# Turning x on VectorE and by DMA instead of on TensorE ahead of an attention layer, with pairs of batches sharing q and k

## The chip, the cores and the metric

The kernel runs on one core of a Trainium2 chip. The metric is the time of one execution in device microseconds (us); times below are medians of several executions. Profiles are single executions of the same programs. An engine's queue that issues transfers is written with a q: SPq is the queue of SyncE, which issues nearly all DMA transfers here, one after the other and in the order of the program.

## The reference, cut to what matters

128 batches of 128 nodes with 512 features (fp32) go through four graph layers, each with a residual and a normalisation. Layer 2 needs x in rows; layer 3 is masked attention with 8 heads, and needs x turned, features on the partitions, for its products with `w_qkv`.

```python
x = _layernorm(x + L0(x))             # adj @ x @ weight + bias
x = _layernorm(x + L1(x))             # graph attention
x = _layernorm(x + L2(x))             # max over nodes
qkv = (x @ w_qkv).reshape(b, n, 3, H, hd).transpose(2, 0, 3, 1, 4)   # layer 3
attn = softmax(where(mask == 0, -inf, q @ k.T * scale))
o = (attn @ v) @ w_proj + b_proj
x = _layernorm(x + o + layernorm(o) * gamma + beta)
```

## The kernel before

A batch is a chain of steps written as a Python generator. A small scheduler (`Plan`) knows a modelled duration of each step and the number of buffers of each kind, and emits the instructions in the order in which its model says they can start; so the order on every engine is fixed when the kernel is built, and a wrong modelled duration gives an order in which something waits. Ranks decide between steps that could start together; the last four batches are ranked 16 ahead, so that they do not end together with nothing beside them.

The steps that matter: layer 3's x is turned on TensorE, four 128x128 transposes per batch, and copied out by ScalarE. Four batches (`G`) share a tile `xT`, so that a q or k product has 512 columns.

```python
G = 4
BUFS = {..., "xT": 1, "v": 8, "qkT": 2, "pr": 2, "pt": 1, "prT": 2, ...}
...
    def query_key(gr, c):                  # 8 of these per group
        yield gr.turned
        ...
        p = product(lambda k: wqkv_sb[:, k, c * P : (c + 1) * P], lambda k: gr.xT[:, k, :])
...
    def batch(i):
        ...                                # layers 0 to 2
        p = bank([P, K, P], "tr")
        for k in range(K):
            nc.tensor.transpose(p[:, k, :], xb[:, k * P : (k + 1) * P], ident)
        yield use("ACT", 0.6, urgent=True)
        nc.scalar.copy(gr.xT[:, :, b * P : (b + 1) * P], p)
        ...
        # softmax: pr on VectorE and ScalarE, turned as 32x32 blocks into pt,
        # written to DRAM (p_d) and read back (prT) through SyncE
        scratch = dram.tile([P, Q, H * S], F32, name="p_d")
        yield use("SP", 0.1, late=2.8)
        to_rows(pt..., scratch)
        bt = yield use("SP", 0.1, "prT", late=4.0)
        from_rows(prT, scratch)
```

The softmax already uses the detour that the change gives to x: a blockwise turn on VectorE, then a DMA to DRAM and back that puts the blocks in place.

## Time and profile before

| | before |
|---|---|
| time, median of 3 | 3414.68 us (3414.14 to 3414.78) |
| TensorE busy | 3378.9 us, 99% |
| TensorE idle (span 3412.8 less busy) | 33.9 us |
| VectorE busy | 76% |
| share of the DMA engines | 19.5% |

The end of the kernel, TensorE in order of time (start us, us, what, and in brackets the idle time ahead of it and what ended it):

```profile
3378.09 1.98 PE L600 MATMUL tr<-prT,v 128*64 128x128 f32 x16 [3.13 <-DMA prT<-p_d]
3381.73 5.17 PE L195 MATMUL mm<-wproj_sb,oT 128*128 128x512 f32 x8 [1.67 <-ACT oT L609]
3388.61 3.70 PE L195 MATMUL mm<-wproj_sb,oT 128*128 128x512 f32 x8 [0.69 <-ACT oT L609]
```

The reader is to see two things: the last batches wait for their own softmax and copies, since nothing else is left to do; and after the wait of 3.13 us the same work takes longer, 5.17 us where the next eight products take 3.70.

### The profile page before, as it was taken

Reading aid. Unit: us, or ns where it says so; the run is one execution under the profiler, and the core shown is the slowest. Engines: PE = TensorE matmul, PEld = TensorE weight load, DVE = VectorE, ACT = ScalarE, POOL = GpSimd, SP = SyncE. Lnnn points to the kernel's source line nnn. Section 1 sums busy time; section 2 is a strip of 40 time slices with the busy share of each in tenths; the row PEclk is TensorE's granted clock in tenths of the full one; section 3 lists DMA queues with packets and bytes.
Section 4 is the critical chain, followed back from the end, with each engine's and each line's share of the span. In section 5 each row is a group of like instructions: output and inputs, shape, how many; then the busy total and the mean of one; then the engine's idle time right before and its main releaser. Section 6 shows DMA issues by size and latency. Waiting matters only on the chain.

```text
span 3412.8 us, 39442 instructions
## 1 busy us (share of the span) xinstructions
PE 3378.9 (99%) x13193; PEld 1727.3 (51%) x13193; DVE 2588.1 (76%) x5399; ACT 1251.9 (37%) x3585; POOL 981.2 (29%) x1031
## 2 busy tenths in 40 slices
PE   9999999999999999999999999999999999999998
PEld 5555555545455455455555555555555545555543
DVE  7776976788777787777877777877778777797766
ACT  3433343334334233342343333433324334244332
POOL 2222422223221333223332223322233222341222
PEclk9999999999999999999999999999999999999999
DMA  4022121202121122111222112221112211121112
GB/s 155 32 86 71 54 75 56 87 30 78 67 77 53 47 78 78 62 60 46 79 76 68 62 48 71 78 68 65 56 56 78 77 60 59 50 78 59 53 69 79
DMA packets 169354, 228.58 MB, mean 67 GB/s; under 512 B 43456, under 2 KB 117312, under 8 KB 169152
## 3 DMA queue, kind: packets, MB, share of 16 engines
q1 hardware_dynamic: 169152, 226.08, 19.5%
q8 instruction: 104, 1.70, 0.2%
q14 instruction: 98, 0.80, 0.1%
HBM read 116.98 MB, written 109.05 MB: 66 GB/s over the span
## 4 chain that ended last, share of the span: by engine, by line
PE 92%; DVE 7%; issue 1%; DMA 0%; ACT 0%; POOL 0%; SPq 0%; POOLq 0%; DVEq 0%; ACTq 0%
PE mm L195 73%; PE tr L203 6%; PE sc L553 4%; PE tr L600 4%; PE mm L515 3%; PE tr L534 2%; DVE st L161 1%; DVE scr L488 1%; DVE x L182 0%; DVE x L507 0%; DVE mv L163 0%; DVE x L481 0%; PE tr L380 0%; DVE x L506 0%; DVE ve L165 0%
## 5 line engine op out<-in xcount | busy, mean ns | idle before, releaser
L195 PE MATMUL mm<-w_sb,yT 128*128 128x512 f32 x2048 | 921.0, 595 | 0.5 <-ACT yT L206 0.5
L195 PE MATMUL mm<-xT,wqkv_sb 128*128 128x512 f32 x2048 | 898.7, 594 | 5.2 <-DVE x L481 2.9
L168 POOL TENSOR_TENSOR rstd<-ve,neghalf 128x1 f32<-128x1 f32 x640 | 446.4, 698 | 1268.5 <-DVE ve L165 1103.3
L195 PEld LDWEIGHTS mm<-xT,wqkv_sb 128*128 128x128 f32 x2048 | 384.7, 190 | 468.5 <-issue 447.0
L195 PEld LDWEIGHTS mm<-w_sb,yT 128*128 128x128 f32 x2048 | 375.5, 190 | 410.4 <-issue 398.1
L195 PE MATMUL mm<-wqkv_sb,xT 128*128 128x512 f32 x1024 | 467.2, 599 | 0.0
L195 PE MATMUL mm<-wproj_sb,oT 128*128 128x512 f32 x1024 | 458.1, 596 | 3.8 <-ACT oT L609 3.8
L188 POOL TENSOR_TENSOR x<-x,beta_sb 128x512 f32<-128x512 f32 x128 | 186.0, 1463 | 937.4 <-PE tr L534 937.4
L571 ACT ACTIVATE pr<-pr,nmx 128x128 f32<-128x128 f32 x1024 | 398.8, 394 | 137.3 <-DVE nmx L567 137.2
L161 DVE BATCH_NORM_STATS2 st<-x 128x6 f32<-128x512 f32 x512 | 349.9, 683 | 4.7 <-ACT x L522 3.4
L177 ACT ACTIVATE x<-x,nmr,rstd 128x512 f32<-128x512 f32 x256 | 206.0, 810 | 288.1 <-DVE nmr L175 284.2
L195 PEld LDWEIGHTS mm<-wproj_sb,oT 128*128 128x128 f32 x1024 | 191.8, 191 | 234.5 <-issue 227.6
L560 DVE TENSOR_TENSOR pr<-sc,maskb 128x1024 f32<-128x1024 f32 x128 | 156.6, 1224 | 191.0 <-PE sc L553 185.3
L195 PEld LDWEIGHTS mm<-wqkv_sb,xT 128*128 128x128 f32 x1024 | 187.0, 190 | 208.7 <-issue 200.6
L442 DVE COPY qkT<-mm 128x512 f32<-128x512 f32 x128 | 87.3, 682 | 247.4 <-PE mm L195 247.2
L206 ACT COPY yT<-tr 128x512 f32<-128x512 f32 x256 | 148.3, 584 | 292.6 <-PE tr L203 290.8
L188 POOL TENSOR_TENSOR x<-x,o 128x512 f32<-128x512 f32 x128 | 180.2, 1408 | 153.6 <-DVE o L617 153.1
L440 ACT ACTIVATE qkT<-mm 128x512 f32<-128x512 f32 x128 | 75.4, 589 | 383.0 <-PE mm L195 383.0
L488 DVE SCALAR_TENSOR_TENSOR scr<-x,wa_rows 128x512 f32<-128x512 f32 x256 | 200.5, 783 | 9.4 <-ACT x L177 3.0
L188 POOL TENSOR_TENSOR x<-x,bias_sb 128x512 f32<-128x512 f32 x128 | 176.7, 1387 | 67.8 <-PE tr L203 57.1
L571 ACT ACTIVATION_READ_ACCUMULATOR pr<-pr,nmx 128x1 f32 x1024 | 195.3, 191 | 0.0
L609 ACT COPY oT<-tr 128x512 f32<-128x512 f32 x128 | 75.0, 586 | 273.4 <-PE tr L600 273.2
(65 smaller groups left out, 3753.6 us busy)
## 6 DMA issues: line engine op xcount, KB each, us to landing
p_d<-pt SPq DMA_DIRECT2D x128, 512.0 KB, 2.6
prT<-p_d SPq DMA_DIRECT2D x128, 512.0 KB, 3.7
x<-in_x SPq DMA_DIRECT2D x128, 256.0 KB, 2.6
out<-x SPq DMA_DIRECT2D x128, 256.0 KB, 2.0
e_d<-et SPq DMA_DIRECT2D x64, 128.0 KB, 1.7
eT<-e_d SPq DMA_DIRECT2D x64, 128.0 KB, 2.2
wqkv_sb<-in_L_gnn_w_qkv SPq DMA_DIRECT2D x1, 3072.0 KB, 10.8
w_sb<-in_L_gnn_weight SPq DMA_DIRECT2D x1, 1024.0 KB, 5.7
```

Of the source, the lines that this page charges most:

```text
L161: nc.vector.bn_stats(st, src)
L168: nc.gpsimd.tensor_tensor(rstd, ve, neghalf, op=ALU.pow)
L177: nc.scalar.activation(xb, xb, AF.Identity, bias=nmr, scale=rstd)
L188: nc.gpsimd.tensor_tensor(dst, dst, other, op=ALU.add)
L195: nc.tensor.matmul(p, lhs(k), rhs(k), start=(k == 0), stop=(k == K - 1))
L203: nc.tensor.matmul(p[:, k, :], xb[:, k * P : (k + 1) * P], nodes, start=True, stop=True)
L206: nc.scalar.copy(yT, p)
L488: nc.vector.scalar_tensor_tensor(scr, xb, 1.0, wa_rows[:, j, :], op0=ALU.mult, op1=ALU.mult, accum_out=gr.s[:, b, j : j + 1],)
L553: nc.tensor.matmul(sc[:, j, c, :], gr.qkT[rws, c, nodes], gr.qkT[rws, K + c, nodes], start=True, stop=True,)
L560: nc.vector.tensor_tensor(pr, sc.rearrange("p j c m -> p (j c) m"), maskb[:, None, :].to_broadcast([P, H, P]), op=ALU.add,)
L571: nc.scalar.activation(pr[:, j, :], pr[:, j, :], AF.Exp, bias=nmx[:, j : j + 1], accum_out=sums[:, j : j + 1],)
L600: nc.tensor.matmul(p[j * HD : (j + 1) * HD, c, :], valued.v[:, (2 * c + j) * HD : (2 * c + j + 1) * HD], prT[:, j * K + c], start=True, st ...
```

## The change

The intent is to take 512 transposes off the engine that is busy 99% of the time. VectorE turns x as 32x32 blocks (`nc.vector.transpose`), SyncE writes the result to DRAM (256 KB) and reads it back in four transfers of 64 KB whose runs are 128 bytes; so the features arrive in another order on the partitions, and the rows of `w_qkv` are loaded in that order too. At the same time groups shrink from four batches to two: `xT` is half as large and gets two buffers, and the q and k products have 256 columns, two in one bank. The diff, cut to its core:

```diff
-G = 4
+G = 2
-    ... "xT": 1, "v": 8, "qkT": 2, "pr": 2, "pt": 1, "prT": 2, ...
+    ... "xT": 2, "v": 8, "qkT": 3, "pr": 2, "pt": 1, "xt": 2, "prT": 2, ...
-        matrix(wqkv_sb, w_qkv)
+        for q in range(Q):
+            nc.sync.dma_start(
+                wqkv_sb[q::Q], w_qkv[q * P : (q + 1) * P].rearrange("(k r) o -> r k o", r=S)
+            )
...
-        p = product(lambda k: wqkv_sb[:, k, c * P : (c + 1) * P], lambda k: gr.xT[:, k, :])
+        p = bank([P, 2, G * P], "mm")
+        for j in range(2):
+            for k in range(K):
+                nc.tensor.matmul(
+                    p[:, j, :], wqkv_sb[:, k, (c + j) * P : (c + j + 1) * P], gr.xT[:, k, :], ...)
...
+    def features(xt, bt, gr, b):
+        scratch = dram.tile([P, Q, P], F32, name="x_d", bufs=8)
+        yield use("SP", 0.1, late=2.3)
+        to_rows(xt, scratch)
+        give(bt)
+        got = yield use("SP", 2.0, lambda: () if gr.xT else ("xT",), late=5.0)
+        ...
+        for a in range(Q):
+            at = b * P + a * S
+            nc.sync.dma_start(
+                gr.xT[:, :, at : at + S],
+                scratch[a * S : (a + 1) * S].rearrange("r q (k s) -> (r q) k s", k=K),
+            )
+        done(gr.turned)
...
-        for k in range(K):
-            nc.tensor.transpose(p[:, k, :], xb[:, k * P : (k + 1) * P], ident)
-        yield use("ACT", 0.6, urgent=True)
-        nc.scalar.copy(gr.xT[:, :, b * P : (b + 1) * P], p)
+        bt = yield use("DVE", 0.65, "xt")
+        xt = buf([P, Q, P], "xt")
+        nc.vector.transpose(xt.rearrange("p q f -> p (q f)"), xb)
+        plan.start(features(xt, bt, gr, b), i)
```

More of the change, by code (lines that the diff above doesn't have):

```diff
@@ L30 @@
     "tr": 3, "mm": 3, "sc": 1,
-    "x": 16, "yT": 3, "e": 2, "et": 1, "eT": 2, "ex": 2, "xT": 1, "v": 8, "qkT": 2,
-    "pr": 2, "pt": 1, "prT": 2, "oT": 2, "o": 2,
+    "x": 16, "yT": 3, "e": 2, "et": 1, "eT": 2, "ex": 2, "xT": 2, "v": 8, "qkT": 3,
+    "pr": 2, "pt": 1, "xt": 2, "prT": 2, "oT": 2, "o": 2,
 }
@@ L273, in loads @@
         landing(bias0_in, P)
-        for i in range(2, G):
+        for i in range(2, 4):
             yield from load(i)
@@ L281, in loads @@
         plan.start(logit_rows(a_sb, slot), 0)
-        for i in range(G, 2 * G):
+        for i in range(4, 8):
             yield from load(i)
@@ L289, in loads @@
         landing(scalars_in, 2 * P)
-        for i in range(2 * G, 3 * G):
+        for i in range(8, 12):
             yield from load(i)
         yield use("SP", 2.5)
-        matrix(wqkv_sb, w_qkv)
+        for q in range(Q):
+            nc.sync.dma_start(
+                wqkv_sb[q::Q], w_qkv[q * P : (q + 1) * P].rearrange("(k r) o -> r k o", r=S)
+            )
         matrix(wproj_sb, w_proj)
@@ L297, in loads @@
         landing(w3_in, (4 * K + 3) * P)
-        for i in range(3 * G, NB):
+        for i in range(12, NB):
             yield from load(i)
@@ L351, in __init__ @@
             self.attention = [Event() for _ in range(G // 2)]
-            self.turned, self.qk = Event(G), Event(2 * K)
+            self.turned, self.qk = Event(G), Event(K)
             self.eT, self.xT, self.qkT, self.slot, self.left = {}, None, None, {}, {}
@@ L367, in group @@
                 plan.start(attention1(groups[g], h), g * G + 2 * h - (16 if g * G >= NB - 4 else 0))
-            for n in range(2 * K):
-                plan.start(query_key(groups[g], n // 2 + K * (n % 2)), g * G + n / (2 * K) - (16 if g * G >= NB - 4 else 0))
+            for n in range(K):
+                plan.start(query_key(groups[g], n // 2 * 2 + K * (n % 2)), g * G + n / K - (16 if g * G >= NB - 4 else 0))
         return groups[g]
@@ L435, in query_key @@
             bp = got
-        p = product(lambda k: wqkv_sb[:, k, c * P : (c + 1) * P], lambda k: gr.xT[:, k, :])
-        gr.read("xT", G + 2 * K)
+        p = bank([P, 2, G * P], "mm")
+        for j in range(2):
+            for k in range(K):
+                nc.tensor.matmul(
+                    p[:, j, :], wqkv_sb[:, k, (c + j) * P : (c + j + 1) * P], gr.xT[:, k, :],
+                    start=(k == 0), stop=(k == K - 1),
+                )
+        gr.read("xT", G + K)
         yield use("ACT" if c < K else "DVE", 0.69, urgent=True)
+        dst = gr.qkT[:, c : c + 2, :]
         if c < K:
-            nc.scalar.mul(gr.qkT[:, c, :], p, HD**-0.5)
+            nc.scalar.mul(dst, p, HD**-0.5)
         else:
             nc.vector.tensor_copy(
-                gr.qkT[:, c, :].rearrange("p (b c r) -> p b c r", b=G, c=Q),
-                p.rearrange("p (b r c) -> p b c r", b=G, c=Q),
+                dst.rearrange("p j (b c r) -> p (j b) c r", b=G, c=Q),
+                p.rearrange("p j (b r c) -> p (j b) c r", b=G, c=Q),
             )
@@ L459, in values @@
         give(bp)
-        gr.read("xT", G + 2 * K)
+        gr.read("xT", G + K)
         event.slot = bv
         done(event)
+    def features(xt, bt, gr, b):
[4 more added lines that the diff above has]
+        got = yield use("SP", 2.0, lambda: () if gr.xT else ("xT",), late=5.0)
+        if gr.xT is None:
+            gr.slot["xT"] = got
+            gr.xT = buf([P, K, G * P], "xT")
+        for a in range(Q):
[3 more added lines that the diff above has]
+                scratch[a * S : (a + 1) * S].rearrange("r q (k s) -> (r q) k s", k=K),
+            )
+        done(gr.turned)
     def batch(i):
@@ L523, in batch @@
         yield from layernorm_dve(xb)
-        got = yield use("PE", 0.5, lambda: ("tr",) if gr.xT else ("tr", "xT"), late=0.2, urgent=True)
-        if gr.xT is None:
-            bt, gr.slot["xT"] = got
-            gr.xT = buf([P, K, G * P], "xT")
-        else:
-            bt = got
-        p = bank([P, K, P], "tr")
-        for k in range(K):
-            nc.tensor.transpose(p[:, k, :], xb[:, k * P : (k + 1) * P], ident)
-        yield use("ACT", 0.6, urgent=True)
-        nc.scalar.copy(gr.xT[:, :, b * P : (b + 1) * P], p)
-        give(bt)
-        done(gr.turned)
+        bt = yield use("DVE", 0.65, "xt")
+        xt = buf([P, Q, P], "xt")
+        nc.vector.transpose(xt.rearrange("p q f -> p (q f)"), xb)
+        plan.start(features(xt, bt, gr, b), i)
         biased = Event()
```

## The prediction

> **What bounds the kernel now.** I read the page's busy shares first, then the chain that ended last, then the groups of TensorE by form, then TensorE in order of time over one group of four batches.
>
> ```profile
> PE 3378.9 (99%) x13193; PEld 1727.3 (51%) x13193; DVE 2588.1 (76%) x5399; ACT 1251.9 (37%) x3585; POOL 981.2 (29%) x1031
> PE 92%; DVE 7%; issue 1%; DMA 0%; ACT 0%; POOL 0%; SPq 0%; POOLq 0%; DVEq 0%; ACTq 0%
> ```
>
> TensorE is busy 99% of the span and is 92% of the chain, so time saved on any other engine is worth nothing, and time saved on TensorE counts in full as long as nobody makes it wait. A busy matmul is not one at its peak, so I need the time that each instruction really takes up on the engine.
>
> ```profile
> L195 PE MATMUL mm<-xT,wqkv_sb 128*128 128x512 f32 x2048 | 898.7, 594 | 5.2 <-DVE x L481 2.9 <-DVE qkT L442 1.5 <-ACT xT L536 0.8
> L534 PE MATMUL tr<-ident,x 128*128 128x128 f32 x512 | 73.1, 276 | 0.0
> L600 PE MATMUL tr<-prT,v 128*64 128x128 f32 x2048 | 140.9, 280 | 3.1 <-DMA prT<-p_d 3.1
> ```
>
> The means (594 and 276 ns) are latencies of overlapped instructions. The distance from start to start is what counts; it is read from the timeline of TensorE (start us, us, what):
>
> ```profile
> 1730.61 3.70 PE L195 MATMUL mm<-w_sb,yT 128*128 128x512 f32 x8
> 1734.14 1.04 PE L534 MATMUL tr<-ident,x 128*128 128x128 f32 x8
> 1735.02 3.60 PE L195 MATMUL mm<-w_sb,yT 128*128 128x512 f32 x8
> 1738.55 1.09 PE L600 MATMUL tr<-prT,v 128*64 128x128 f32 x16
> ...
> 1754.07 0.66 PE L534 MATMUL tr<-ident,x 128*128 128x128 f32 x4
> 1754.56 3.60 PE L195 MATMUL mm<-w_sb,yT 128*128 128x512 f32 x8
> ...
> 1768.76 3.60 PE L195 MATMUL mm<-w_sb,yT 128*128 128x512 f32 x8
> 1772.19 1.02 PE L515 MATMUL mm<-x,adjT 128*128 128x512 f32 x2
> ...
> 1782.60 0.60 PE L534 MATMUL tr<-ident,x 128*128 128x128 f32 x4
> 1783.03 3.60 PE L195 MATMUL mm<-w_sb,yT 128*128 128x512 f32 x8
> ```
>
> Eight 512-column instructions take 1772.19 - 1768.76 = 3.43 us: 0.429 each. Eight transposes take 1735.02 - 1734.14 = 0.88 and four 0.43: 0.109 each. Beside a score or value product, which uses half the array (64 rows or columns), a run is 0.1 us longer: 1738.55 - 1735.02 = 3.53. So each change between half-array and full-array products costs 0.1 us. No idle time stands in these lines. The pattern repeats every 105.16 us (the chain's long runs start at 1266.16, 1371.33, 1476.50): four batches.
>
> **What the Trainium skill says.** (1) "TensorE: Matmul & The Clock Gate", section "Back-to-back issue gap", gives N/2.4 + 2.5 ns for an isolated warm matmul, and "FP8 and Floating Point Precision", section "TensorE Precision Notes", gives four passes for true fp32. The trace agrees: a product counts as two instructions of 429 ns, 858 ns in all, four times 214.5 (512/2.4 + 2.5 is 215.8). So halving the columns halves the time but for a few ns. (2) The same first page, "Part 4: PE-mode transpose", has about 275 ns in context for a transpose, output in PSUM, so a copy must follow. The trace has 276 ns as latency but 109 ns of engine time; the smaller number is what removing it is worth. The copy is ScalarE's, L536, 71.4 us, off the path. (3) "VectorE: DVE Perf Modes", "The three transpose paths": VectorE turns 32x32 blocks only. That is why blocks must then be carried by DMA; the trace has its 128x1024 turn at 1239 ns. (4) "DMA: Bandwidth & Descriptors", "Why small descriptors are slow (HBM only)": a fixed cost per packet. In the trace, alone in a window of 2.32 us, one 256-byte-run read shows
>
> ```profile
> q1 hardware_dynamic: 528, 0.13, 24.8%
> eT<-e_d SPq DMA_DIRECT2D x1, 128.0 KB, 2.3
> ```
>
> that is 0.248 x 2.32 x 16 / 528 = 17 ns of one engine per packet, where 256 bytes at the 22.5 GB/s per engine of the first 20 us (324 GB/s at 90% busy) would need 11. A fixed part of about 6 ns is seen.
>
> **The change part by part.**
> TensorE, removed: 512 transposes x 0.109 = 55.8 us. All of it lies on the path.
> TensorE, changed: q and k come from 1024 products of 512 columns before, 2048 of 256 after; in instructions 2048 x 0.429 = 879 us against 4096 of a size not in the trace. From 0.109 at 128 columns and 0.429 at 512 the straight line gives 0.2157 at 256: 883.5. Cost +4.5 us. Weight loads double for this part, but one takes 190 ns beside a 216 ns slot, so it stays hidden.
> TensorE, order: the built programs show 510 changes between half-array and full-array products before and 438 after, as two groups interleave. 72 x 0.1 = -7.2 us.
> The sum on TensorE is -55.8 + 4.5 - 7.2 = -58.5 us. As a check, the slots of all instructions of the program before add up to 3367 us, against 32 x 105.16 = 3365; the other 46 us of the span are start, end and a lower clock there, and I leave them as they are.
> VectorE: +128 turns of 128x512. From 311 ns (128 elements) and 1239 (1024) a line gives 0.71 us: +91 us, 76% to 79%. The qkT copies stay 128 of 512 elements. ScalarE: -71 us. The turn stands behind the last normalisation of layer 2, where the TensorE transpose stood.
> DMA: per batch one 256 KB write (a store of that size lands in 2.0 us) and four reads of 64 KB, each 512 runs of 128 bytes. With about 15 ns a packet (17 less half of the 256 bytes' own time, a little rounded up for reads of HBM) that is 2048 x 15 / 16 = 1.9 us on all engines, with the write 2.7 us, of 26 us per batch: the DMA share goes from 20% to about 30%. An issue takes 0.37 us, so four take 1.5.
>
> **Whether this latency is hidden.** The new chain is: last product of layer 2, rest of layer 2, turn, write, reads. Before, TensorE turned x as little as 8.1 us (by the slots in the built order) after the L515 product of the same batch without waiting, so the first stretch is at most that. Add 0.7 for the turn, 2.3 for the write with its issue, 1.1 + 2.2 + about 1 for four reads: 15.4 us. From the built program I added the slots of all TensorE instructions between the last L515 product of each pair and its first q/k product: 18.3 us at the least through the steady part, mostly 22 to 45. So it is hidden, with 3 us to spare at the tightest. Only the second last pair has 8.6 us: there TensorE will stand still for about 7 us. The final batches give a little back: before, the four that end together wait 3.1 + 1.7 + 3 x 0.7 us; now two end together, which saves perhaps 2. Scattered waits from busier DMA queues and VectorE: I allow 3 us. Total of new waits +8.
>
> 3414.7 - 58.5 + 8 = 3364 us, 1.5% faster.
>
> **Rivals.** (a) The reads land late: with 128-byte runs twice as slow as I think, the chain grows by 3 to 4 us, the tight pairs (one in seven, about nine in all) wait a few us each, and the value products wait if the softmax reads queue behind. What speaks for it: the softmax chain has at least 20.7 us of TensorE work to hide in after, 23.0 before, and its median landing is already 3.7 us. Against: DMA idle 80% of the time, and the margin. It would make 3375 to 3420. (b) VectorE becomes a second bound: 79% is an average, and it evicts k, the products of two layers and the scores. For it: between 20 and 128 us of the trace it is 93 to 96% busy already. Against: before, TensorE waited on VectorE for about 10 us in all. It would add 10 to 30 us. (c) The SyncE queue blocks: it issues in order, and a read into an xT buffer still in use holds up the softmax transfers behind it. The built program has such places (two buffers now, each half as big). It looks like (a) in time, but the queue's wait is for TensorE. (d) The 0.109 is too small, because a run of transposes also breaks a run of matmuls; the lines show none of it (1783.03 to 1786.47 is again 3.44), so a gain over 68 us (2%) needs something I do not see.
>
> **Range and chances.** The floor is no new wait at all and a better end: 3350. Waits as in (b) or half of (a) give 3385. So 3347 to 3388. Faster by over 2% means under 3346.4: 18 us better than my sum, 8%. Slower by over 2% needs (a) or (c) in full, over 120 us of waits: 4%.
>
> **What would show it.** Right: no transposes into tr from x; the q/k group with 4096 instructions at 0.215 us from start to start; the same four batches in 103.4 us; TensorE idle still under 40 us; DMA share near 30%, VectorE near 79%. Wrong: a start-to-start distance of 0.25 or more at 256 columns (weight loads seen, +140 us); idle on TensorE put down to DMA xT or DMA prT (rivals a, c), or to VectorE copies (b); or a span under 3346, which would mean that the transposes cost more than their slots.

## The result, and the profile after

| | before | after |
|---|---|---|
| time, median of 4 runs each | 3414.73 us (3414.14 to 3417.1) | 3365.37 us (3363.78 to 3367.79) |
| ratio | | 0.9855, 95% interval 0.9838 to 0.9872 |
| span of the profiled run | 3412.8 us | 3366.0 us |
| TensorE busy / idle | 3378.9 / 33.9 us | 3324.6 / 41.4 us |

The changed kernel is 1.4% faster; the time predicted was 3364.

The page of the changed kernel: busy time, the chain that ended last, the DMA queue (packets, MB, share), and the transfers concerned (count, size, median us from issue to landing):

```profile
PE 3324.6 (99%) x14729; PEld 2070.5 (62%) x14729; DVE 2669.9 (79%) x5527; ACT 1189.7 (35%) x3457; POOL 923.1 (27%) x1031
...
q1 hardware_dynamic: 457968, 293.23, 29.0%
...
PE 90%; DVE 6%; DMA 2%; issue 1%; SPq 0%; ACT 0%; POOL 0%; POOLq 0%; DVEq 0%; ACTq 0%
...
L442 PE MATMUL mm<-xT,wqkv_sb 128*128 128x256 f32 x4096 | 918.2, 381 | 8.8 <-DVE st L161 8.8
...
prT<-p_d SPq DMA_DIRECT2D x128, 512.0 KB, 3.8
...
xT<-x_d SPq DMA_DIRECT2D x512, 64.0 KB, 2.5
```

TensorE is still busy 99% and 90% of the chain: the bound has not moved. Its busy time fell by 54.3 us and its idle time rose by 7.5, which gives the 46.8 us between the spans (the profiled execution after is the slowest of its four, 3367.79 us; the medians differ by 49.4). The softmax's reads land as fast as before (3.8 us against 3.7).

The 256-column products from start to start, TensorE in order of time:

```profile
1789.51 3.62 PE L442 MATMUL mm<-xT,wqkv_sb 128*128 128x256 f32 x16
1792.96 0.38 PE L383 MATMUL tr<-ident,s 128*128 128x128 f32 x2
```

Sixteen take 1792.96 - 1789.51 = 3.45 us, 0.216 each: half of the 0.429 of 512 columns and hardly more, so the doubled weight loads stay hidden.

The detour of x, hidden. This is a place of the steady part with the least TensorE work to hide behind, first TensorE, then VectorE, then SyncE's queue:

```profile
1629.43 1.02 PE L543 MATMUL mm<-x,adjT 128*128 128x512 f32 x2
...
1641.55 7.03 PE L195 MATMUL mm<-w_sb,yT 128*128 128x512 f32 x16
...
1648.64 3.62 PE L442 MATMUL mm<-xT,wqkv_sb 128*128 128x256 f32 x16
```

```profile
1636.43 0.70 DVE L556 STREAM_TRANSPOSE xt<-x 128x512 f32<-128x512 f32 x1
```

```profile
1637.16 0.32 SPq L212 DMA_DIRECT2D x_d<-xt  x1
1639.14 2.55 SPq L486 DMA_DIRECT2D xT<-x_d  x4
```

The last product of layer 2 ends at 1630.29 (the next group starts there), the turn starts 6.1 us later, the write is issued at 1637.16 and the four reads from 1639.14 on. The fourth is issued at 1641.06 and lands 2.50 us later by the trace, at 1643.56. TensorE needs it at 1648.64, 5.1 us after, and does not wait. Note the 2.55 us: four reads of 64 KB hold the queue of SyncE for that long.

By the landing of the last read, other places are tighter, for all that they have more TensorE work. One of them, with products that need `xT` at 2257.64 (TensorE, SyncE's queue, TensorE):

```profile
2229.89 1.98 PE L543 MATMUL mm<-x,adjT 128*128 128x512 f32 x4
```

```profile
2250.29 2.55 SPq L486 DMA_DIRECT2D xT<-x_d  x4
```

```profile
2257.64 3.62 PE L442 MATMUL mm<-xT,wqkv_sb 128*128 128x256 f32 x16
```

The first two of the four L543 instructions are the last product of layer 2 of this pair, done at some 2230.9. VectorE turns x only at 2247.13, 16.3 us later, and the last read lands at 2254.72, 2.9 us ahead of the products; from 128 to 3200 us the trace has one margin that is smaller, 1.7 us ahead of the products at 269.20.

The end of the changed kernel, TensorE in order of time:

```profile
3278.04 16.80 PE L442 MATMUL mm<-xT,wqkv_sb 128*128 128x256 f32 x64 [8.79 <-DVE st L161]
...
3348.39 1.98 PE L619 MATMUL tr<-prT,v 128*64 128x128 f32 x16 [5.99 <-DMA prT<-p_d]
3351.09 5.77 PE L195 MATMUL mm<-wproj_sb,oT 128*128 128x512 f32 x8 [0.73 <-ACT oT L628]
```

Here the detour is not hidden. The wait of 8.79 us is put down to VectorE by the profile, but a q/k product needs `xT`, the last read of it lands at 3277.80 by the trace, 0.24 us before the products start, and the wait goes away when just these batches are turned without the detour (experiment 9). And the 64 products behind it take 16.80 us where 64 x 0.216 = 13.8 would do: the wait costs nearly 3 us more after it is over.

### The profile page after: what moved, and what is told of

It reads as the page before. It is cut to its first block, busy times and chain, and to the rows that moved or that the text cites. A ratio compares the mean times of both kernels' runs of the same rounds, so it can differ in the third digit from the quotient of the medians.

```text
span 3366.0 us, 43501 instructions
## 1 busy us (share of the span) xinstructions
PE 3324.6 (99%) x14729; PEld 2070.5 (62%) x14729; DVE 2669.9 (79%) x5527; ACT 1189.7 (35%) x3457; POOL 923.1 (27%) x1031
## 4 chain that ended last, share of the span: by engine, by line
PE 90%; DVE 6%; DMA 2%; issue 1%; SPq 0%; ACT 0%; POOL 0%; POOLq 0%; DVEq 0%; ACTq 0%
PE mm L195 47%; PE mm L442 27%; PE tr L203 6%; PE sc L572 4%; PE tr L619 4%; PE mm L543 3%; DVE st L161 1%; DMA p_d<-pt 1%; DMA prT<-p_d 1%; DVE scr L516 1%; DVE x L648 1%; PE tr L383 0%; SPq L486 0%; DVE t L645 0%; DVE x L182 0%
## 5 line engine op out<-in xcount | busy, mean ns | idle before, releaser
L442 PE MATMUL mm<-xT,wqkv_sb 128*128 128x256 f32 x4096 | 918.2, 381 | 8.8 <-DVE st L161 8.8
L442 PEld LDWEIGHTS mm<-xT,wqkv_sb 128*128 128x128 f32 x4096 | 771.4, 190 | 138.3 <-issue 20.6
L168 POOL TENSOR_TENSOR rstd<-ve,neghalf 128x1 f32<-128x1 f32 x640 | 406.6, 635 | 1100.6 <-DVE ve L165 996.9
L195 PEld LDWEIGHTS mm<-w_sb,yT 128*128 128x128 f32 x2048 | 383.3, 191 | 453.3 <-issue 441.6
L188 POOL TENSOR_TENSOR x<-x,beta_sb 128x512 f32<-128x512 f32 x128 | 167.1, 1307 | 177.1 <-DVE xt L556 131.2
L468 ACT COPY v<-mm 128x512 f32<-128x512 f32 x128 | 74.9, 585 | 347.7 <-PE mm L195 347.5
L450 ACT ACTIVATE qkT<-mm 128x512 f32<-128x512 f32 x128 | 76.1, 594 | 341.2 <-PE mm L442 341.0
L182 DVE TENSOR_SCALAR x<-x,mv,rstd 128x512 f32<-128x512 f32 x256 | 172.5, 676 | 14.4 <-POOL rstd L168 14.0
```

The costliest lines, as they stand in the source:

```text
L168: nc.gpsimd.tensor_tensor(rstd, ve, neghalf, op=ALU.pow)
L182: nc.vector.tensor_scalar(xb, xb, mv[:, 0:1], rstd, op0=ALU.subtract, op1=ALU.mult)
L188: nc.gpsimd.tensor_tensor(dst, dst, other, op=ALU.add)
L195: nc.tensor.matmul(p, lhs(k), rhs(k), start=(k == 0), stop=(k == K - 1))
L442: nc.tensor.matmul(p[:, j, :], wqkv_sb[:, k, (c + j) * P : (c + j + 1) * P], gr.xT[:, k, :], start=(k == 0), stop=(k == K - 1),)
```

## The experiments

Theory T: the gain is the transposes' own time on TensorE, 0.109 us each, and the detour is hidden. Rivals: the pairs do the work (R1); the detour has no margin and sits on an edge (R2), with two versions of it: the length of the chain, or the time that the reads take of SyncE's queue, which holds up the softmax's transfers behind them.

### 1. Each transpose twice, in the kernel before

```diff
-        for k in range(K):
-            nc.tensor.transpose(p[:, k, :], xb[:, k * P : (k + 1) * P], ident)
+        for _ in range(2):
+            for k in range(K):
+                nc.tensor.transpose(p[:, k, :], xb[:, k * P : (k + 1) * P], ident)
```

> The kernel before with each of the 512 transposes of x done twice into the same place, nothing else changed. If a transpose costs its 0.109 us of TensorE and nothing more, +56 us: 3466 to 3475 us. If part of them ran in time that was idle anyway: under 3455. If a run of transposes costs more than its slots (breaking a run of matmuls, longer eviction): over 3480.

3464.18 us, ratio 1.0145 (1.0131 to 1.0159), 2 us under the range expected. The page:

```profile
PE 3434.6 (99%) x13705; PEld 1784.4 (52%) x13705; DVE 2592.0 (75%) x5399; ACT 1267.3 (37%) x3585; POOL 979.8 (28%) x1031
```

TensorE's busy time rose from 3378.9 to 3434.6 us: 55.7 us for 512 more transposes, 0.109 each. The time rose by less than expected, since idle time fell by 5.3 us (33.9 to 28.6). The first term of the prediction stands: the slot of a transpose is 0.109 us and lies on the path.

### 2. The pairs alone

The kernel before, with `G = 2`, two `xT` and three `qkT` buffers and products of two times 256 columns; x is still turned on TensorE.

```diff
-G = 4
+G = 2
-    ... "xT": 1, "v": 8, "qkT": 2, ...
+    ... "xT": 2, "v": 8, "qkT": 3, ...
     # query_key as in the change; no turn on VectorE, no detour
```

> The kernel before with groups of two, TensorE still turning x. My sum: 4096 instructions of 256 columns at 0.2157 us for 2048 at 0.429: +4.5 us; 456 changes between half-array and full-array products in the built program for 510: -5.4 us; so 3405 to 3416 us, with the end of the program giving or taking a few us. Rival, that the gain comes from sharing q and k by two (shorter waits, another order) and not from the turn: under 3390 us. Rival, weight loads show at 256 columns: over 3440 us.

3410.72 us, ratio 0.9988 (0.9976 to 1.0001). TensorE is busy 3378.3 us, 0.6 less than before. By the prediction's terms it should be +4.5 for 256 columns and, with 456 changes between half-array and full-array products instead of 510, -5.4: a sum of -0.9. R1 falls: pairs by themselves gain next to nothing (0.1%).

### 3. The detour alone

The changed kernel with groups of four again, as before the change; a second `xt` buffer does not fit beside the larger tiles.

```diff
-G = 2
+G = 4
-    ... "xT": 2, "v": 8, "qkT": 3, "pr": 2, "pt": 1, "xt": 2, ...
+    ... "xT": 1, "v": 8, "qkT": 2, "pr": 2, "pt": 1, "xt": 1, ...
     # query_key with 512 columns; turn on VectorE and detour kept
```

> The changed kernel with groups of four as before, turn on VectorE and DMA (one buffer for the turned blocks, as two do not fit beside the larger groups). My sum: 512 transposes at 0.109 us away, -55.8; the 510 changes between half-array and full-array products stay; the built program leaves at least 18 us of TensorE work between the last layer-2 product of a group and its first q/k product, except in the last group, where it leaves none and the chain of 15 us shows: about +15. So 3365 to 3380 us. Rival, that the latency is hidden only because pairs need fewer batches: waits in each of 32 groups, over 3400 us. Rival, the gain belongs to the pairs: 3405 us and up.

3420.6 us, ratio 1.0017 (1.0004 to 1.003). A clear miss: all the transposes are gone and nothing is gained. TensorE's busy time fell by 39.3 us and not by 55.8, and its idle time went from 33.9 us to 80.8. Of that, 32 us lie between 128 and 3200 us, above all as waits for the softmax's reads (13 waits, 29.4 us in the whole run), and 41 us after 3200; of these 14.6 are the one wait for `xT` that was expected at the end (about 15). A wait in the middle, SyncE's queue and then TensorE:

```profile
2686.29 0.83 SPq L212 DMA_DIRECT2D p_d<-pt  x1
2687.16 6.04 SPq L479 DMA_DIRECT2D xT<-x_d  x8
2693.25 0.62 SPq L216 DMA_DIRECT2D prT<-p_d  x1
```

```profile
2697.98 1.98 PE L612 MATMUL tr<-prT,v 128*64 128x128 f32 x16 [3.02 <-DMA prT<-p_d]
```

The write of the softmax is issued at 2686.29 and by the trace lands 3.9 us later, at 2690.17. Its read could go then. But eight reads of x stand ahead of it and are issued until 2693.20, so it goes at 2693.25, 3.1 us late, and TensorE waits 3.02 us. Of the 13 waits nine have such a late read, by 2.6 to 3.9 us. The transfers themselves are slower in these nine as well: 3.1 to 3.9 us to landing for the write (median of the run 2.7) and 4.1 to 5.0 for the read (3.8), so the queue is the larger part of the delay and not all of it. In groups of four such bunches are frequent: counted over all 512 reads of x in the trace, a window of 12 us that starts at a read holds 12 reads or more in 60 cases, up to 16; in the changed kernel in one case, with 12. So neither part of the change gains alone, 3410.7 and 3420.6, and together they give 3365.4.

### 4. Only one turned tile in the changed kernel

Experiment 3 had one `xt` buffer instead of two, so this is taken alone.

```diff
-    ... "pt": 1, "xt": 2, ...
+    ... "pt": 1, "xt": 1, ...
```

> The changed kernel with one buffer for the turned blocks in place of two, as the run of the turn alone had to have. If this single buffer was no part of its loss: 3362 to 3372 us. If it was: 3385 us and up.

3366.11 us, ratio 0.9857 (0.9842 to 0.9872): no difference. The buffer is not what experiment 3 lost by.

### 5. The detour alone, with the scheduler told a longer issue

If the queue is the cause, a plan that knows how long four reads hold it (2.55 us, not 2.0) should avoid the waits.

```diff
 # against experiment 3
-        got = yield use("SP", 2.0, lambda: () if gr.xT else ("xT",), late=5.0)
+        got = yield use("SP", 2.6, lambda: () if gr.xT else ("xT",), late=5.0)
```

> The turn alone in groups of four, with the planner told that four block reads take 2.6 us of SyncE's queue, as measured, and not 2.0, so that it puts more TensorE work in front of what stands behind them. Theory of the queue: TensorE's idle time between 128 and 3200 us falls from 32 to under 15; the end may grow, as the last group of four still has nothing to hide behind: 3395 to 3425 us in all. Rival, the waits are contention of the transfers and have nothing to do with the planned queue time: idle time stays near 30.

3407.35 us, ratio 0.9977 (0.9962 to 0.9992), in the range. TensorE busy in two stretches of the middle, 1138 and 1634 us long, experiment 3 and then this one (window, its length, then TensorE's busy time and instructions):

```profile
128.00:1266.00 1138.00, 1123.39 (x4255) 563.48 (x4254) 890.81 (x1831) 399.02 (x1168) 304.92 (x337) 1.00 0.29 87
1266.00:2900.00 1634.00, 1618.87 (x6196) 818.49 (x6195) 1308.22 (x2689) 587.53 (x1710) 451.46 (x496) 1.00 0.29 85
```

```profile
128.00:1266.00 1138.00, 1134.47 (x4350) 570.04 (x4349) 896.77 (x1838) 404.36 (x1199) 306.67 (x336) 1.00 0.29 86
1266.00:2900.00 1634.00, 1630.74 (x6233) 822.01 (x6232) 1317.27 (x2726) 584.54 (x1693) 467.44 (x514) 1.00 0.30 88
```

Idle time falls from 14.6 + 15.1 to 3.5 + 3.3 us: with the issue planned at its true length the middle's waits nearly vanish. The bunches do not: 53 windows of 12 us still hold 12 reads or more, up to 16. So a bunch costs little where the plan knows its length. (The number changes the order on all engines, so this run alone does not part the queue from a luckier order; experiment 8 keeps the order.) What is left is the drain: from 2900 us on TensorE is idle for about 60 us, against 43 in experiment 3, so the part of the expectation that idle time before 3200 falls below 15 us failed (27 us). Of the 42 us between this run and the changed kernel, 35 are this idle time (60.8 against 25.8 us), so the longer drain is the larger part of what groups of four lose here. Why a group of four drains so badly was not tried further.

### 6. The reads issued by ScalarE

```diff
-            nc.sync.dma_start(
+            nc.scalar.dma_start(
                 gr.xT[:, :, at : at + S],
```

This was done to the changed kernel and to the detour alone, in the unchanged order. For the changed kernel:

> The changed kernel with its block reads issued from ScalarE's queue, order on the other engines the same. Theory: in pairs SyncE's queue delays little (8 us of idle time on TensorE between 128 and 3200 us), so 3356 to 3367 us. Rival, ScalarE, which now stands 2.5 us per batch in issues, is late with evictions that TensorE waits for: over 3372 us. Rival, the queue costs much in pairs too: under 3352 us.

3388.63 us, ratio 0.992 (0.9905 to 0.9935), a miss: it is what the rival of ScalarE's late work was to give. For the detour alone:

> The turn alone in groups of four, with one thing changed: the four reads of the turned blocks are issued from ScalarE's queue and not from SyncE's. The order on TensorE, VectorE and GpSimd is the same, instruction for instruction. Theory, in the run of the turn alone the softmax reads were issued late because they stand behind 4 to 8 block reads of 0.63 us each in SyncE's queue: TensorE's idle time between 128 and 3200 us, 32 us there, falls under 12; the idle end of 42 us stays; 3390 to 3403 us. Rival, the transfers themselves are slower beside each other, or the landing of the blocks is what is late: idle time stays, 3415 us and up.

3457.46 us, ratio 1.0119, a miss. In both, the reads wait for their data at the head of ScalarE's own work, as the waits of the changed kernel's variant show (waiting line, releaser, us in total, times, longest):

```profile
ACT x L177 <- DMA xT<-x_d: 113.9, 19, 13.3
```

In the second variant TensorE's waits for the softmax's reads did fall, from 29.4 to 17.3 us, but ScalarE's own delays outweigh it. SyncE is better suited for these reads, as it has nothing else to do; on whether the queue is the cause the pair is inconclusive.

### 7. One more trip in the chain

A further copy from DRAM to DRAM between write and reads lengthens the chain of every batch.

```diff
         to_rows(xt, scratch)
+        again = dram.tile([P, Q, P], F32, name="x_d2", bufs=8)
+        nc.sync.dma_start(again, scratch)
+        scratch = again
```

> The changed kernel with one more copy of 256 KB from DRAM to DRAM in every batch between the write of the turned blocks and their reads, the planned order untouched: the chain grows by 2.5 to 3 us, DMA share by about 4 points. Theory, latency hidden with 4 to 5 us to spare in the tightest pair of the steady part and shown only at the end: 3366 to 3376 us. Rival, the schedule is at its edge and each us of DMA shows in the tight pairs and in the softmax transfers queued behind: 3385 us and up.

3406.7 us, ratio 0.998 (0.9964 to 0.9995). A miss: I expected the margin to swallow it, and 41 us came, most of it as idle time of TensorE (41.4 to 76.1 us), waiting for `xT` (8.4 us in all), for `eT` of layer 1 (11.3) and for others; the longest wait, 15.0 us, lies near the end. The waits of SyncE's queue tell why even transfers of other layers are hit:

```profile
SPq L480 <- DMA x_d<-xt: 261.2, 128, 4.1
...
SPq L489 <- DMA x_d<-x_d: 224.6, 96, 3.2
```

The added copy waits at the head of the queue for the write before it, 2.0 us per batch, and the reads then for the copy. An in-order queue makes everything behind wait too. So this experiment lengthens the chain and holds the queue at once, and does not tell the two versions of R2 apart. It shows that R2 is close.

### 8. Four more issues, read by nobody

To hold the queue without lengthening the chain, four transfers per batch were added that nobody waits for; first as tiny copies of 512 bytes:

```diff
+        for _ in range(Q):
+            nc.sync.dma_start(dram.tile([P, 1], F32, name="none", bufs=32), scratch[:, 0, 0:1])
         done(gr.turned)
```

> The changed kernel with four tiny copies (512 bytes each, read by nobody) issued after the block reads of every batch; planned order untouched. They lengthen no chain of the batch itself; they only take about 1.3 us per batch of SyncE's queue and its completion counters. Theory, what made the extra trip cost 41 us is SyncE's queue, in order, in which the transfers of other batches stand behind: 3378 to 3400 us, with waits on prT, eT and xT. Rival, only the latency of the blocks' own chain matters: 3363 to 3369 us.

4517.47 us, ratio 1.3221. This is a flawed experiment: the copies are 128 runs of 4 bytes, and other transfers landed late beside them. In one place the reads of `xT` went 11.9 us after the write that they wait for (2.0 in the changed kernel), at a DMA share of only 33%. It says nothing on the queue. So the transfers were made harmless, 64 KB in runs of 512 bytes into on-chip tiles that nobody reads, on top of experiment 4:

```diff
+        for _ in range(Q):
+            nc.sync.dma_start(work.tile([P, P], F32, name="none", bufs=4), scratch[:, 0])
         done(gr.turned)
```

> The changed kernel with one turned tile instead of two (which alone cost nothing) and, after the block reads of every batch, four more reads of 64 KB in runs of 512 bytes from a DRAM tensor into on-chip tiles that nobody reads. They are in no chain of data: they only take the SyncE queue's time, some 0.3 to 0.6 us each, so 1.3 to 2.4 us per batch of 26, and 3 points of DMA share. If the in-order SyncE queue is what makes the carried turn dear where its issues bunch up: 3375 to 3395 us, with waits of TensorE on prT, eT or xT spread over the middle. Rival, only the latency of the blocks' own chain matters and the queue has time to spare: 3363 to 3370 us and no new waits.

3443.32 us, ratio 1.008 (1.0063 to 1.0096): 77 us more than experiment 4. The queue theory is right in kind, and its cost was put far too low. SyncE and then TensorE at one of 12 waits for `prT`:

```profile
1777.73 0.32 SPq L212 DMA_DIRECT2D p_d<-pt  x1
1778.15 3.49 SPq L486 DMA_DIRECT2D xT<-x_d  x4
1781.69 2.04 SPq L491 DMA_DIRECT2D none<-x_d  x4
1783.77 2.54 SPq L486 DMA_DIRECT2D xT<-x_d  x4
1786.36 2.04 SPq L491 DMA_DIRECT2D none<-x_d  x4
1788.45 0.43 SPq L216 DMA_DIRECT2D prT<-p_d  x1
```

```profile
1792.61 1.58 PE L621 MATMUL tr<-prT,v 128*64 128x128 f32 x16 [4.38 <-DMA prT<-p_d]
1794.12 8.29 PE L195 MATMUL mm<-wproj_sb,oT 128*128 128x512 f32 x16
```

The write of the softmax goes at 1777.73 and by the trace lands 4.7 us later, at 1782.41 (median 2.6); its read goes at 1788.45, 6.0 us after it could. In eight of the 12 waits the read goes 6.0 to 7.9 us after the landing of the write; in the whole changed kernel it never does so by more than 3.2 us. The longest of the 12, 12.65 us at the end, is not new (12.76 in experiment 4). The transfers themselves are in general no slower than in the changed kernel (medians: `prT` 3.8 us, `xT` 2.4), and the added ones hold the queue for 2.0 us per batch. So in these eight the order and length of issues, not the engines that move the data, make the wait.

The 77 us come in two parts, against experiment 4: idle time of TensorE rose by 52.0 us (42.7 to 94.7), and its busy time by 25.5 (3321.8 to 3347.3) for the same instructions. The second part is the clock. Two windows of 2 us behind that wait (the last three columns are the granted clock, DMA share and GB/s):

```profile
1794.00:1796.00 2.00, 2.00 (x5) 0.84 (x4) 0.00 (x0) 1.77 (x8) 0.00 (x0) 0.50 0.32 74
1796.00:1798.00 2.00, 2.00 (x6) 0.95 (x5) 0.00 (x0) 1.13 (x6) 0.00 (x0) 0.88 0.54 188
```

After a wait of 4.38 us TensorE runs at half clock for some 3 to 4 us, and 16 products take 8.1 us instead of 6.9. The Trainium skill says so on "TensorE: Matmul & The Clock Gate", "Part 1: The HAM clock gate": an idle window of about 3.4 us halves the clock, until about 3.4 us of sustained work release it. The trace agrees on the half, 0.50. Waits of 2.1 and 2.7 us in experiment 3 were already followed by slow products (16 value products in 1.51 and 1.97 us instead of 1.09), though one of 2.99 us in the same run was not (1.09 us); and after the 8.79 us at the end of the changed kernel the clock stays at 0.50 for over 5 us.

### 9. Two other ends

The wait of 8.79 us lies at the end, where the last four batches have run ahead and the batches 120 to 123 have nothing beside them. First these four are turned on TensorE again, after a copy on VectorE that puts the features in the permuted order:

```diff
+        if NB - 8 <= i < NB - 4:
+            nc.vector.tensor_copy(
+                xt.rearrange("p k (r q) -> p k r q", q=Q), xb.rearrange("p (q k r) -> p k r q", q=Q, k=K))
+            ...
+            for k in range(K):
+                nc.tensor.transpose(p[:, k, :], xt[:, k, :], ident)
+            ...
+        else:                      # as in the change
```

> The changed kernel with the four batches that come last (120 to 123) turned by TensorE again, after a copy by VectorE that puts their columns in the permuted order; all others as in the change. Theory: of the 26 us that TensorE stands idle after 3200 us, the 8.8 us wait for the last pairs' blocks shrinks to 2 or 3 and the slow clock behind it (16.8 us for 64 products that take 13.8 elsewhere) goes: 3354 to 3361 us. Rival, the softmax chain sets the end whatever the blocks do: 3363 us and up.

3360.1 us, ratio 0.9839 (0.9824 to 0.9853). The q/k products of that place now wait 0.73 us, and a transpose 0.89, in place of 8.79: it was the detour that the end waited for. Then only the ranks were changed in the changed kernel, six batches put 8 ahead instead of four put 16 ahead:

```diff
-            plan.start(batch(i), i if i < NB - 4 else i - 16)
+            plan.start(batch(i), i if i < NB - 6 else i - 8)
     # and likewise for the two kinds of steps that a group starts
```

> The changed kernel with its last six batches ranked 8 places ahead instead of the last four ranked 16 ahead (the ranking was chosen for groups of four). Theory, what is left of waits lies in the end, because too little work is left beside the last pairs: TensorE's idle time after 3200 us falls from 26 to about 12, 3347 to 3358 us. Rival, the end cannot be filled by another order: 3362 us and up.

3347.12 us, ratio 0.9802 (0.9787 to 0.9816): the fastest kernel, some 18 us better than the change. After 3200 us TensorE waits twice, 0.74 us each time, and a tail of some 11 us follows the last product (10 before). The first of the two, TensorE in order of time:

```profile
3329.09 3.70 PE L195 MATMUL mm<-wproj_sb,oT 128*128 128x512 f32 x8 [0.74 <-ACT oT L628]
```

The waits of 8.79 and 5.99 us are gone, and with them the slow products (3.70 us again for eight). Whether such a retuning would also help the kernel before was not run. The prediction took a span under 3346 us as a sign that a transpose costs more than its slot; this run, at 3347, shows that the order at the end can bring a span as short.

## Why the prediction was right, point by point

**The transposes, -55.8 us, on the path.** Confirmed: experiment 1 gives +55.7 us of busy time for as many again.

**Products of 256 columns, +4.5; fewer changes of array half, -7.2.** The slot was put at 0.2157 us and is 0.216. Experiment 2 gives -0.6 us for both together where the terms give -0.9. A term of this size cannot be told from others more closely.

**The sum on TensorE, -58.5.** Measured -54.3 on the page, and in the steady part: 14 batches take 362.0 us (the pattern starts at 1626.00 and again at 1988.01), 25.86 each against 105.16 / 4 = 26.29, which is -0.43, or -55.3 us for 128. The sum was about 3 us too large; which term that is stays open.

**VectorE at 79% and DMA near 30%.** 79% and 29.0%. The packet of 15 ns was rounded up by more than "a little" (17 less half of 11 is 11 to 12 ns): the DMA engines took 2.4 us more per batch, (0.290 x 3366.0 - 0.195 x 3412.8) / 128, where 2.7 were reckoned. Rival (b), VectorE as a second bound, did not come: the turns take 0.70 us each as estimated, and TensorE has no new steady wait for VectorE.

**The latency, 15.4 us of 18.3 at the tightest.** The place with the least TensorE work measures 1648.64 - 1630.29 = 18.35 us, against about 13.3 used. The term for the issues was wrong, though: 0.37 us each, four in 1.5, was read from transfers that stand alone; behind one another the reads of x take 0.63 us, 2.55 for four. The stretch ahead of the turn was quicker there, 6.1 us against at most 8.1, which covered it. But "at most 8.1" does not hold elsewhere, as VectorE has other work in between: ahead of the products at 2257.64 that stretch took 16.3 us, the chain 23.9 of 26.8 us. A margin of 3 us was told and 2.9 us is there, but in another place and for another reason, so the number is in part luck.

**New waits, +8.** Idle time rose by 7.5. The composition fits less well than the sum. The second last pair waits 8.79 us for the 7 predicted, and loses 3 more to the half clock, for which the prediction had no term. The 2 us that the final batches were to give back did not come: 1.0 + 6.0 + 0.7 us of waits against 3.1 + 1.7 + 3 x 0.7 before. The scattered waits are 1.9 us between 1266 and 2900 us, all for the softmax's reads and each under 0.7 us, within the 3 us allowed. Rival (a) did not come. Rival (c) came in the queue but not on TensorE: SyncE waits 11 times, 31.6 us in all and up to 12.9, until TensorE has done with an `xT`. The longest of these ends at 3097, and TensorE itself has no wait of more than 0.7 us between 1266 and 3200 us.

**What the prediction had not seen.** It treated the pairs as a small item (4.5 - 7.2 us on TensorE) and rival (c), the queue, as a thing of 4% together with (a). With the pairs' finer turns, two batches at a time, the reads hardly bunch; without them the gain is lost, to waits in the middle and at the end where the issue is planned too short (experiment 3), and to the end where it is not (experiment 5); and 2 us more of queue time per batch turn a gain of 49 us into a loss of 28 (experiment 8). The result was as told, but one reason given against these rivals, DMA engines idle 80% of the time, was the wrong reading: the queue in front of them has its own time, and issues wait in it in order. That the pairs act through the bunching and not through the two smaller `xT` buffers is not shown: both come with the pairs, the bunches alone cost little in experiment 5, and the bunch shown in experiment 3 begins after SyncE has waited 1.7 us for a free `xT` (over the run 12 such waits, 18.7 us, against the 31.6 us of the changed kernel).

## What to carry to other kernels

Taking work off the busiest engine gains what its slots take up from start to start (here 0.109 us, not the 0.276 of the record's latency), but a detour by DMA is paid for in the issuing queue: count the time that its issues hold an in-order queue, look at which transfers stand behind them, and tell the scheduler that length. The same transfers were cheap where they were spread or where the plan knew their length, and dear where it did not. And a wait of TensorE of more than some 2 to 4 us can cost more than its length, as the clock was halved behind many such waits; so look last at the end of the kernel, where waits cannot be hidden and a change of order alone was worth 18 us.

## What the Trainium skill lacked or had wrong

- "TensorE: Matmul & The Clock Gate", "Part 4: PE-mode transpose" gives about 275 ns for a transpose (of bf16). Here, in fp32, 276 ns is the latency of one; what a run of them takes up is 0.109 us each (experiment 1: 55.7 us for 512).
- The same page, Part 1, has an idle window of about 3.4 us before the clock halves. Here waits of 2.1 and 2.7 us were already followed by slow products, and one of 2.99 us was not (experiment 3). The length agrees: by the clock records of the changed kernel's trace the half clock lasts 3.41 us at 634.9 and 10.24 us, three times that, from 3273.4, 4.1 us into the wait of 8.79.
- "DMA: Bandwidth & Descriptors", "Latency and other measured facts" has no time for which an issue holds the queue of SyncE (the page's part on trn3 counts sequencer cycles per instruction for earlier chips too, but not by what stands ahead or by the runs). Here it is 0.32 to 0.38 us for a transfer alone, and 0.51 (runs of 512 bytes) to 0.63 us (runs of 128 bytes) where four go behind one another, in one place 0.87; 2.0 us more of it per batch cost 77 us (experiment 8).
- The same page says of transfers under 512 bytes that they are slow, but not that others land late beside them: 512 added copies of 512 bytes in 4-byte runs cost 1151 us, (4517 - 3366) / 512 = 2.2 us each, at a DMA share of 33%.
